# Two attention layers on one core: warm-up products on the raw image, and a stage's statistics spread over six steps

## The chip, the cores and the metric

The kernel runs on one core of one Trainium2 chip. The metric is the device time of one execution in microseconds (us). A core has five engines with queues of their own: TensorE (PE in the profile, with its weight loads shown apart as PEld), VectorE (DVE), ScalarE (ACT), GpSimd (POOL) and SyncE (SP, which only issues transfers here). Each works through its own list of instructions; they meet through semaphores. All arithmetic is fp32.

## The reference, cut to what matters

Four images of 32 x 32 pixels and 768 channels pass through two attention layers. Before each layer the image is normalised over groups of channels, and that normalisation is what the change touches:

```
def _gn(v, G=32, eps=1e-5):
    B_, H_, W_, C_ = v.shape
    g = v.reshape(B_, H_, W_, G, C_ // G)
    m = jnp.mean(g, axis=(1, 2, 4), keepdims=True)
    s = jnp.var(g, axis=(1, 2, 4), keepdims=True)
    return ((g - m) / jnp.sqrt(s + eps)).reshape(v.shape)
...
x = x + _L0_conv_ref(_gn(x), ...)
x = x + _L1_conv_ref(_gn(x), ...)
```

`_L0_conv_ref` is attention with 12 heads of 64 channels over the 1024 pixels, with a relative position bias from rows and columns, between projections (q, k, v and the output). `_L1_conv_ref` is the same, with a 3 x 3 depthwise convolution and a layer norm on q, k and v ahead of the scores.

## The kernel before

**Stages, items and steps.** A stage is one layer of one image; there are eight, in the order image 0 layer 0, image 1 layer 0, image 0 layer 1, image 1 layer 1, and then the same for images 2 and 3. A stage has six items, a pair of heads each. `attend` (L700) makes the attention of one item: for each of two halves of the queries (`c`) it goes twice over four tiles of 128 keys (`g`). For such a group PE makes four tiles of scores (L785 q by k, L787 the bias added), ACT takes their exponentials into `e` (L792), and PE multiplies them with v (L809). In layer 0 DVE also adds the four `e` into `acc` (L801, L803), whose column sums PE makes later (`z`, L754); in layer 1 the sums come out of the product with v itself.

**Who orders the work.** Nothing is scheduled by the compiler on PE, DVE, ACT and POOL: each engine executes in the order in which the program is written. `attend` is a generator which yields twice after a group's scores, exponentials and additions, and twice after its products with v. Each yield is a step; an item has 16. Everything else (the next item's projections, the convolution's taps, weight sums, the next image's normalisation) is cut into pieces which `at(step, piece)` hangs on steps (L943); the loop at L1001 writes the pieces of a step between two parts of `attend`. A step thus sets a place in every engine's list, and not a time: engines reach their parts of one step at different times.

In one item the steps 8 and 9 come after the scores of the third group, 10 and 11 after its products with v, 12 and 13 after the scores (and, in layer 0, the four additions to `acc`) of the fourth group, and 14 and 15 after that group's products with v.

**The normalisation.** `group_norm` (L301) is a generator too. For each of six slices `xn[:, n, :]` of the image (128 partitions x 1024) it issues two `bn_stats` on DVE (L307), 512 columns each. `bn_aggr` makes mean and variance per partition from them (L311, tile `mv`). A PE product with a constant matrix averages over the four partitions of a channel group (L316, `gn_mean`); DVE copies it out of PSUM (L318, `gmean`) and makes the group's variance term (L320, L321, `gd`), PE averages that (L325, `gn_var`), DVE adds epsilon (L327), and ACT and DVE make one over the root (L153 to L160). Last, six DVE instructions normalise the image in place (L337).

For the first image the whole generator runs ahead of the loop (L994). For the other seven stages, `k` = 1 to 7, it runs in the third item of the stage before (L952): twelve calls, three steps apart, from step 2 of that item on. The generator before yields after slices 1 and 3, after the aggregate, and again idly, so that the steps of that item are

| part | step |
|---|---|
| `bn_stats` of slices 0, 1 (four instructions) | 2 |
| slices 2, 3 (four) | 5 |
| slices 4, 5 (four) and the aggregate | 8 |
| mean product L316, L318 to L321 | 14 |
| variance product L325, L327 | 20 |
| one over the root | 23 |
| normalising, two slices each | 26, 29, 32 |

For `k` = 1, 2, 5, 6 the surrounding stage is of layer 0, for `k` = 3, 4, 7 of layer 1.

**The start.** The first image comes in as six transfers, one a slice (L228). Behind the variance product PE executes five "warm" products (L333) of the identity with a constant of 384 columns, whose result nobody reads; then the first projection (L131, `qkv`) waits for the normalised slices. A full fp32 product shows in the trace as two matmul records and two weight loads.

Of the kernel before, what the change touches and what calls it, by code (L numbers as in the profile page):

```python
# [9 lines left out]
F32 = mybir.dt.float32  # L10
# [3 lines left out]
ALU = mybir.AluOpType  # L14
# [3 lines left out]
P = 128  # L18
# [4 lines left out]
NC = C // P  # L23
# [5 lines left out]
EPS = 1e-5  # L29
# [16 lines left out]
def two_layers(ctx: ExitStack, tc: tile.TileContext, keep, x_in, wqkv, wproj, rels, windows, vrow, small, const, onehot, picks, out):  # L46
# [19 lines left out]
    nc = tc.nc  # L66
# [8 lines left out]
    ps_a = pool("ps_a", 1, space=PSUM)  # L75
# [49 lines left out]
    def small_bank(name):  # L125
        return ps_small.tile([P, 512], F32, tag="small", name=name)
# [14 lines left out]
    cst = fixed.tile([P, NCONST], F32, tag="cst", name="cst")  # L141
    nc.sync.dma_start(cst, const)
    ident = cst[:, IDENT : IDENT + P]
# [6 lines left out]
    def rsqrt(v, n, name):  # L150

        ln = stat.tile([P, n], F32, tag=f"ln{n}", name=f"ln_{name}")
        nc.scalar.activation(ln, v, AF.Ln)  # L153
        r = stat.tile([P, n], F32, tag=f"r{n}", name=f"r_{name}")
        nc.scalar.activation(r, ln, AF.Exp, scale=-0.5)
        t = stat.tile([P, n], F32, tag=f"t{n}", name=f"t_{name}")
        nc.vector.tensor_mul(t, r, r)
        nc.vector.tensor_mul(t, t, v)
        nc.vector.tensor_scalar(t, t, -0.5, 1.5, ALU.mult, ALU.add)
        nc.vector.tensor_mul(r, r, t)  # L160
        return r


    stages = [(b0 + k, layer) for b0 in range(0, B, 2) for layer in range(2) for k in range(2)]
# [42 lines left out]
    def shift(i):  # L207

        return 4 if i and items[i][1] == 0 and items[i - 1][1] == 1 else 0
# [3 lines left out]
    for i, (_, layer, hp) in enumerate(items):  # L213
        first = (i - 1) * 16 + shift(i)
# [8 lines left out]
    def load_xn(stage):  # L223
        b, layer = stage
        xn = xnp.tile([P, NC, T], F32, tag=f"xn{stages.index(stage) % 2}", name="xn")
        src = rows(mid[b] if layer else x_in[b])
        for n in range(NC):
            nc.sync.dma_start(xn[:, n, :], src[:, n, :])  # L228
        xns[stage] = xn
# [60 lines left out]
    def mix_tokens(stage):  # L290


        x11, x12, x21, x22 = (xns[stage][:, n : n + 3, h : h + HALF] for n in (0, 3) for h in (0, HALF))
        for to, x, y, op in (
            (quarters[1], x11, x12, ALU.add), (x12, x12, x22, ALU.subtract), (quarters[2], x21, x22, ALU.add),
            (x21, x21, x11, ALU.subtract), (quarters[0], x11, x22, ALU.add),
        ):
            nc.vector.tensor_tensor(to, x, y, op)
            yield

    def group_norm(stage):  # L301

        xn = xns[stage]
        st = stat.tile([P, NC * 2, 6], F32, tag="bn", name="bn", bufs=1)
        for n in range(NC):
            for h in range(2):
                nc.vector.bn_stats(st[:, 2 * n + h, :], xn[:, n, h * HALF : (h + 1) * HALF])  # L307
            if n in (1, 3):
                yield
        mv = stat.tile([P, 2], F32, tag="mv", name="mv")  # L310
        nc.vector.bn_aggr(mv, st.rearrange("p a b -> p (a b)"))  # L311
        yield
        yield
        group = cst[:, GROUP : GROUP + P]
        ps = small_bank("gn_mean")
        nc.tensor.matmul(ps[:, 0:1], group, mv[:, 0:1], start=True, stop=True)  # L316
        mean = stat.tile([P, 1], F32, tag="gmean", name="gmean")
        nc.vector.tensor_copy(mean, ps[:, 0:1])  # L318
        d = stat.tile([P, 1], F32, tag="gd", name="gd")
        nc.vector.tensor_sub(d, mv[:, 0:1], mean)  # L320
        nc.vector.scalar_tensor_tensor(d, d, d, mv[:, 1:2], ALU.mult, ALU.add)  # L321
        yield
        yield
        ps = small_bank("gn_var")
        nc.tensor.matmul(ps[:, 0:1], group, d, start=True, stop=True)  # L325
        v = stat.tile([P, 1], F32, tag="gv", name="gv")
        nc.vector.tensor_scalar(v, ps[:, 0:1], EPS, None, ALU.add)  # L327
        yield
        if stage == stages[0]:

            ps = small_bank("warm")
            for _ in range(5):
                nc.tensor.matmul(ps[:, : 3 * P], ident, cst[:, : 3 * P], start=True, stop=True)  # L333
        r = rsqrt(v, 1, "gn")
        yield
        for n in range(NC):
            nc.vector.tensor_scalar(xn[:, n, :], xn[:, n, :], mean, r, ALU.subtract, ALU.mult)  # L337
            if n % 2:
                yield
# [603 lines left out]
    def at(step, piece):  # L943
        events.setdefault(step, []).append(piece)

    n_steps = NKT * (T // QC)
    oss = [[] for _ in stages]
    for k in range(1, len(stages)):
        first = (k - 1) * NC * n_steps
        at(first + n_steps + 4, lambda k=k: load_xn(stages[k]))  # L950
        norm = group_norm(stages[k])
        for r in range(12):  # L952
            at(first + 2 * n_steps + 2 + 3 * r, lambda norm=norm: next(norm, None))
        if stages[k][1] == 0:
            mix = mix_tokens(stages[k])
            for r in range(5):
                step = 5 * n_steps + r // 3 if stages[k - 1][1] else 4 * n_steps + 4 + r // 2
                at(first + step, lambda mix=mix: next(mix, None))
        elif stages[k - 1][1] == 0:
            at(first + 4 * n_steps + 6, lambda: [nc.gpsimd.memset(pad, 0.0) for pad in pads])  # L960
# [17 lines left out]
    for k, stage in enumerate(stages):  # L978
        call, sums, products = project(stage, oss[k])
        first = (k + 1) * NC * n_steps  # L980
# [13 lines left out]
    for _ in group_norm(stages[0]):  # L994
        pass
# [330 lines left out]
```

## Time and profile before

| | |
|---|---|
| time, median of 3 runs | 3866.32 us (3866.01 to 3870.61) |
| profiled execution, its own time | 3867.89 us |
| its span (first to last instruction) | 3866.1 us |
| ACT busy | 1793.1 us (46%) |
| DVE busy | 2468.8 us (64%) |
| POOL busy | 477.8 us (12%) |
| scores, L785 and L787, PE busy | 815.7 and 615.2 us |
| projections and the like, L131, PE busy | 814.3 us |
| products with v, L809, PE busy | 598.0 us |
| additions to `acc`, L803, DVE | 360.1 us, 1225 ns each |
| `bn_stats`, L307, DVE | 96 instructions, median 677 ns |
| aggregate, L311, DVE | 8 instructions, median 480 ns |

How to read it: a group of instructions stands with its line in the kernel, its engine, what it writes and reads (out<-in), how many there are, their busy time and mean, and the engine's idle time just ahead of them with what ended it. A timeline row has the start in the span, the duration from the first start to the last end of the merged instructions, and in brackets the idle time ahead of the row. On DVE a row's duration overlaps the next row's by some 0.1 us, so that costs are better taken from one start to the next. The profile also has the clock that TensorE was granted, as a share of full speed.

### The profile page before, as it was taken

The page shows a single profiled execution, that of the slowest core. Times are in us where ns is not written, and L with a number is a line of the kernel's source. Part 1 is how long each engine was busy: PE and PEld are TensorE (multiplying, and loading weights), DVE is VectorE, ACT ScalarE, POOL GpSimd, SP SyncE. Part 2 cuts the span into 40 slices and gives each one's busy share as a digit, 9 for nine tenths or more (in the row PEclk, how much of TensorE's full clock was granted, in tenths as well). Part 3 has the DMA queues.
Part 4 walks back from the last instruction along what each step waited for, and adds up shares of the span by engine and source line. Part 5 has one row for each costly group of instructions (what it writes and reads, how often), then busy time and mean ns, then how long its engine had stood idle before and what let it go on. Part 6 is the DMA issues. An engine that isn't in the chain of part 4 may idle for free. (4 is left out here: it accounts for less than half of the span.)

```text
span 3866.1 us, 76044 instructions
## 1 busy us (share of the span) xinstructions
PE 3780.0 (98%) x32988; PEld 1646.0 (43%) x32988; DVE 2468.8 (64%) x3068; ACT 1793.1 (46%) x2573; POOL 477.8 (12%) x870
## 2 busy tenths in 40 slices
PE   8999999999999999999899999999999999999998
PEld 3535535533334443344435445355343444434432
DVE  2566454559588876788354554455685887857774
ACT  2455434545255553456334544254452555525551
POOL 0111100111111211111100010011111121111120
PEclk9999999999999999999999999999999999999999
DMA  4344452321431213311234132522124121142123
GB/s 150 104 121 116 130 159 73 108 71 42 123 96 46 69 43 112 109 45 45 74 113 123 52 77 62 173 62 74 43 55 151 54 66 48 47 123 64 48 53 99
DMA packets 211013, 330.61 MB, mean 86 GB/s; under 512 B 47570, under 2 KB 100562, under 8 KB 210672
## 3 DMA queue, kind: packets, MB, share of 16 engines
q1 hardware_dynamic: 122912, 212.26, 17.6%
q0 software_dynamic: 87760, 113.40, 12.3%
q8 instruction: 263, 4.31, 0.5%
q14 instruction: 78, 0.64, 0.1%
HBM read 184.62 MB, written 40.10 MB: 58 GB/s over the span
## 5 line engine op out<-in xcount | busy, mean ns | idle before, releaser
L792 ACT ACTIVATE e<-s 128x1024 f32<-128x1024 f32 x768 | 773.7, 1024 | 420.9 <-PE s L787 392.4
L785 PE MATMUL s<-q,k 64*128 64x512 f32 x3072 | 815.7, 608 | 18.3 <-ACT e L792 16.6
L131 PE MATMUL qkv<-xn,wqkv_t 128*64 128x512 f32 x3648 | 814.3, 595 | 2.6 <-DVE gmean L318 2.6
L531 DVE SCALAR_TENSOR_TENSOR shared<-shared,sm 128x1056 f32<-128x1056 f32 x576 | 758.1, 1316 | 15.6
L787 PE MATMUL s<-bias,ones 64*128 64x512 f32 x1536 | 615.2, 795 | 14.0 <-DMA bias<-whole 10.2
L809 PE MATMUL av<-e,vt 128*64 128x512 f32 x2624 | 598.0, 597 | 0.0
L627 POOL DMA_DIRECT2D bias<-high x384 | 205.0, 549 | 2174.0 <-ACT high L616 1936.8
L131 PEld LDWEIGHTS qkv<-xn,wqkv_t 128*64 128x64 f32 x3648 | 251.3, 137 | 490.5 <-issue 485.2
L803 DVE TENSOR_TENSOR acc<-acc,e 128x1024 f32<-128x1024 f32 x294 | 360.1, 1225 | 113.7 <-ACT e L792 87.0
L785 PEld LDWEIGHTS s<-q,k 64*128 64x128 f32 x3072 | 281.2, 188 | 279.1 <-issue 208.8
L514 ACT ACTIVATE shared<-qkv,sm 128x512 f32<-128x512 f32 (+1 forms) x288 | 129.3, 502 | 501.3 <-PE qkv L131 501.3
L809 PEld LDWEIGHTS av<-e,vt 128*64 128x64 f32 x2624 | 182.0, 137 | 353.0 <-issue 318.9
L787 PEld LDWEIGHTS s<-bias,ones 64*128 64x128 f32 x1536 | 149.8, 189 | 202.2 <-issue 185.0
L627 POOL DMA_DIRECT2D bias<-whole x384 | 206.2, 560 | 58.4 <-DVE whole L617 45.7
L801 DVE TENSOR_TENSOR acc<-e 128x1024 f32<-128x1024 f32 x49 | 60.0, 1225 | 226.9 <-ACT e L792 216.8
L722 ACT COPY weighed<-av 128x512 f32<-128x512 f32 x96 | 56.4, 587 | 276.9 <-PE av L809 276.9
L546 DVE TENSOR_REDUCE mean<-ln_c 128x8 f32<-128x512 f32 x144 | 98.5, 684 | 117.1 <-PE ln_c L543 117.1
L600 PEld LDWEIGHTS rel<-q,rel 64*32 64x32 f32 x6144 | 112.0, 106 | 78.1 <-issue 72.7
L728 POOL DMA_DIRECT2D z<-weighed x47 | 26.9, 573 | 919.5 <-ACT weighed L722 514.0
L557 DVE TENSOR_REDUCE lnv<-shared 128x16 f32<-128x1024 f32 x72 | 87.6, 1216 | 69.4 <-ACT shared L553 69.4
L600 PE MATMUL rel<-q_t,rel 64*32 64x32 f32 x6144 | 123.6, 195 | 4.2 <-issue 4.2
L399 DVE TENSOR_TENSOR shared<-shared,m3m 128x512 f32<-128x512 f32 x66 | 45.4, 687 | 128.7 <-PE m3m L131 128.4
(158 smaller groups left out, 4471.3 us busy)
## 6 DMA issues: line engine op xcount, KB each, us to landing
bias<-high POOLq DMA_DIRECT2D x384, 128.0 KB, 2.9
bias<-whole POOLq DMA_DIRECT2D x384, 128.0 KB, 3.0
wqkv_t<-in_wqkv SPq DMA_DIRECT2D x78, 384.0 KB, 3.2
wqkv_t<-mixed SPq DMA_DIRECT2D x66, 384.0 KB, 3.1
wproj_t<-mixed SPq DMA_DIRECT2D x48, 384.0 KB, 3.3
wqkv_t<-in_wqkv SPq DMA_DIRECT2D x66, 192.0 KB, 2.5
xn<-in_x SPq DMA_DIRECT2D x24, 512.0 KB, 8.3
x<-in_x SPq DMA_DIRECT2D x48, 256.0 KB, 3.3
```

Of the source, the lines that this page charges most:

```text
L131: nc.tensor.matmul(ps[lo : lo + D], a[:, lo : lo + D], b, start=start, stop=stop, **kw)
L514: nc.scalar.activation(self.pad[s][:, rows, there : there + src.shape[2]], src, AF.Identity, bias=col(self.column(s)))
L531: nc.vector.scalar_tensor_tensor(y, window, tap, y, ALU.mult, ALU.add)
L546: nc.vector.tensor_reduce(of, heads, AX.X, ALU.add)
L557: nc.vector.tensor_reduce(v, squared.rearrange("p (a d) -> p a d", d=D), AX.X, ALU.add)
L600: nc.tensor.matmul(ps[lo : lo + S, k * S : (k + 1) * S].rearrange("p (b c) -> p b c", b=2), rel[rows, 2 * self.layer + i, first : first + ...
L627: nc.gpsimd.dma_start(sets, some.unsqueeze(1).to_broadcast([D // 2, 2, QC]))
L785: nc.tensor.matmul(ps[:, j, :], k[rows, keys], q[rows, cols], start=True, stop=False)
L787: nc.tensor.matmul(ps[:, j, :], ones[rows, keys], bias[c][rows, kt // 2, :], start=False, stop=True,)
L792: nc.scalar.activation(e, ps, AF.Exp)
L803: nc.vector.tensor_tensor(acc, acc, e, ALU.add)
L809: nc.tensor.matmul(av[j * D : (j + 1) * D, :], pair.vt[:, kt, j * D : (j + 1) * D], e[:, j, :], start=(kt == 0), stop=(kt == NKT - 1),)
```

## The change

In `group_norm` the generator now yields after each of the slices 0 to 4, so that the statistics run in six calls of two `bn_stats`, the last one with the aggregate; the two idle yields are gone. The list of steps on which the calls hang is written out. The result: slices 0 to 5 on steps 2, 4, 6, 8, 10 and 12 of the item, the aggregate with slice 5 on step 12 (it was on step 8); mean, variance, root and normalising stay on steps 14, 20, 23, 26, 29, 32.

For the first image the five warm products move and change: three are issued behind the statistics of slice 4 and read that slice of the raw image (so they wait for its transfer), one stands between mean product and variance product, two stand behind the variance product. They are six, and write into a bank of the scores' pool instead of the small bank.

```
             for h in range(2):
                 nc.vector.bn_stats(st[:, 2 * n + h, :], xn[:, n, h * HALF : (h + 1) * HALF])
-            if n in (1, 3):
+            if stage == stages[0] and n == NC - 2:
+
+                ps = ps_a.tile([P, 2, 512], F32, tag="a", name="warm")
+
+                def warm(n):
+                    for _ in range(n):
+                        nc.tensor.matmul(ps[:, 0, : 3 * P], ident, xn[:, NC - 2, : 3 * P], start=True, stop=True)
+
+                warm(3)
+            if n < NC - 1:
                 yield
         mv = stat.tile([P, 2], F32, tag="mv", name="mv")
         nc.vector.bn_aggr(mv, st.rearrange("p a b -> p (a b)"))
         yield
-        yield
         group = cst[:, GROUP : GROUP + P]
-        ps = small_bank("gn_mean")
-        nc.tensor.matmul(ps[:, 0:1], group, mv[:, 0:1], start=True, stop=True)
+        small = small_bank("gn_mean")
+        nc.tensor.matmul(small[:, 0:1], group, mv[:, 0:1], start=True, stop=True)
+        if stage == stages[0]:
+            warm(1)
...
         nc.vector.scalar_tensor_tensor(d, d, d, mv[:, 1:2], ALU.mult, ALU.add)
         yield
-        yield
...
         if stage == stages[0]:
-
-            ps = small_bank("warm")
-            for _ in range(5):
-                nc.tensor.matmul(ps[:, : 3 * P], ident, cst[:, : 3 * P], start=True, stop=True)
+            warm(2)
         r = rsqrt(v, 1, "gn")
...
         norm = group_norm(stages[k])
-        for r in range(12):
-            at(first + 2 * n_steps + 2 + 3 * r, lambda norm=norm: next(norm, None))
+        for r in (0, 2, 4, 6, 8, 10, 12, 18, 21, 24, 27, 30):
+            at(first + 2 * n_steps + 2 + r, lambda norm=norm: next(norm, None))
```

More of the change, by code (lines that the diff above doesn't have):

```diff
@@ L312, in group_norm @@
         yield
-        yield
         group = cst[:, GROUP : GROUP + P]
-        ps = small_bank("gn_mean")
-        nc.tensor.matmul(ps[:, 0:1], group, mv[:, 0:1], start=True, stop=True)
+        small = small_bank("gn_mean")
+        nc.tensor.matmul(small[:, 0:1], group, mv[:, 0:1], start=True, stop=True)
+        if stage == stages[0]:
+            warm(1)
         mean = stat.tile([P, 1], F32, tag="gmean", name="gmean")
-        nc.vector.tensor_copy(mean, ps[:, 0:1])
+        nc.vector.tensor_copy(mean, small[:, 0:1])
         d = stat.tile([P, 1], F32, tag="gd", name="gd")
@@ L322, in group_norm @@
         yield
-        yield
-        ps = small_bank("gn_var")
-        nc.tensor.matmul(ps[:, 0:1], group, d, start=True, stop=True)
+        small = small_bank("gn_var")
+        nc.tensor.matmul(small[:, 0:1], group, d, start=True, stop=True)
         v = stat.tile([P, 1], F32, tag="gv", name="gv")
-        nc.vector.tensor_scalar(v, ps[:, 0:1], EPS, None, ALU.add)
+        nc.vector.tensor_scalar(v, small[:, 0:1], EPS, None, ALU.add)
         yield
         if stage == stages[0]:
-            ps = small_bank("warm")
-            for _ in range(5):
-                nc.tensor.matmul(ps[:, : 3 * P], ident, cst[:, : 3 * P], start=True, stop=True)
+            warm(2)
         r = rsqrt(v, 1, "gn")
```

## The prediction, on record before the changed kernel ran

> **What bounds the kernel now.** I read the page's busy times first, then PE's waits, then the timeline around the two places that the change touches.
>
> ```profile
> PE 3780.0 (98%) x32988; PEld 1646.0 (43%) x32988; DVE 2468.8 (64%) x3068; ACT 1793.1 (46%) x2573; POOL 477.8 (12%) x870
> ```
>
> PE is busy for 3780.0 of 3866.1 us, idle for 86. That alone doesn't prove it the bound, so I looked at what its idle time waits for (engine, line, who released it: total us, times, longest):
>
> ```profile
> PE gn_mean L316 <- DVE mv L311: 17.2, 1, 17.2
> ...
> PE qkv L131 <- DVE gmean L318: 2.6, 3, 0.9
> ```
>
> The first is the start of the program. The statistics cost PE nothing later: `gn_mean` never waits again. Second row: the copy of the mean is late for the next projection three times (at 1197, 1702 and 3113, all in layer 1 stages). Now the place of the seven later normalisations, first stage; PE's timeline, then DVE's:
>
> ```profile
> 252.77 3.65 PE L809 MATMUL av<-e,vt 128*64 128x512 f32 x16
> 256.35 0.38 PE L316 MATMUL gn_mean<-mv,cst 128*128 128x1 f32 x2
> 256.67 1.13 PE L785 MATMUL s<-q,k 64*128 64x512 f32 x4
> ```
>
> ```profile
> 247.41 2.46 DVE L307 BATCH_NORM_STATS2 bn<-xn 128x6 f32<-128x512 f32 x4
> 249.90 0.48 DVE L311 BATCH_NORM_AGGREGATE mv<-bn 128x2 f32<-128x72 f32 x1
> 250.30 0.63 DVE L765 SCALAR_TENSOR_TENSOR t<-t,inv 128x512 f32<-128x512 f32 x1
> ...
> 252.30 1.22 DVE L617 TENSOR_TENSOR whole<-whole,high 128x1024 f32<-128x1024 f32 x1
> 253.43 5.21 DVE L803 TENSOR_TENSOR acc<-acc,e 128x1024 f32<-128x1024 f32 x4
> 258.55 0.15 DVE L318 COPY gmean<-gn_mean 128x1 f32<-128x1 f32 x1
> ```
>
> No row has a bracket: neither engine idles. From 212 to 300 PE has no gap at all, so here a PE delay lengthens the program. And DVE is behind PE: PE's mean product is at 256.35, DVE reaches the same step at 258.55. The product has its aggregate at 250.38, 6 us early, only because the aggregate stands on step 8.
>
> The start, all engines:
>
> ```profile
> 12.75 1.29 DVE L307 BATCH_NORM_STATS2 bn<-xn 128x6 f32<-128x512 f32 x2 [0.20 <-DMA xn<-in_x]
> ...
> 19.37 5.35 PE L333 MATMUL warm<-cst 128*128 128x384 f32 x10 [0.25 <-DVE gv L327]
> ...
> 20.83 4.43 DVE L337 TENSOR_SCALAR xn<-xn,gmean,r_gn 128x1024 f32<-128x1024 f32 x6
> ...
> 24.66 15.67 PE L131 MATMUL qkv<-xn,wqkv_t 128*64 128x512 f32 x72
> ```
>
> The first slice is normalised by 21.57 (six in 4.43, so 0.74 each), but PE is in the warm products until 24.65.
>
> [...] weight loads of the warm products are 0.64 us apart up to 22.74, and 0.32 at the end (the recorded full clock begins at 23.16). [...] Windows (from:to, length, busy us and count by engine, granted clock, DMA):
>
> ```profile
> 1820.00:1825.40 5.40, 3.40 (x216) 2.21 (x216) 5.26 (x5) 3.77 (x8) 0.00 (x0) 1.00 0.05 17
> 1825.40:1828.80 3.40, 3.40 (x65) 2.21 (x66) 3.33 (x5) 3.31 (x6) 0.00 (x0) 0.50 0.02 5
> 1842.50:1849.20 6.70, 6.12 (x20) 3.18 (x20) 6.11 (x9) 3.36 (x5) 3.66 (x7) 0.50 0.74 176
> ```
>
> A gap of 2.00 us before 1825.32 was followed by 3.4 us at 0.50; the gap of 3.80 before 1843.08 by 6.8 us at 0.50, from 0.6 before its end. Gaps of 1.57 (1535), 1.76 (880) and one of 2.21 (1860) left the clock full.
> [...] At the start load and product of `gn_mean` both wait until 17.25[...].
> [...] The DVE rows above run in the order of the program.
>
> **The change, part by part.**
>
> *Statistics while a layer 0 stage runs (k = 1, 2, 5, 6).* In DVE's list, slices 4, 5 and the aggregate leave the place after the third group's additions; slice 3 stays there; slice 4 goes between L772 and L617; slice 5 and the aggregate go behind the four additions of the fourth group, immediately ahead of L318. No transfers hang on them; the lists of ACT, POOL and SP stay as they are, and PE's changes at the start alone. From one start to the next, four `bn_stats` and the step to the aggregate take 2.49 (247.41 to 249.90), two in front of an aggregate therefore 1.30 (1.2, and 0.1 for its wait).
> At 247.41: two `bn_stats` (1.23, half of 2.46) and the aggregate (0.40, from 249.90 to 250.30) are gone: L765 starts 1.63 earlier, at 248.7. Slice 4 takes back 1.2, so L617 and the additions start 0.43 earlier, at 253.0; their exponentials (ACT 249.62 to 253.91) are in time for that. The additions take 5.12 from start to next start: 258.12. Slice 5: 259.42. Aggregate 0.48: 259.90; 0.06 from aggregate to product, as at the start (17.19 to 17.25): **`gn_mean` starts at 259.96 instead of 256.35, and PE waits 3.6 us**.
> The same arithmetic elsewhere: L318 follows PE's product by 2.20 (697.13, 699.33), 2.19 (2173.85, 2176.04) and 2.18 (2613.62, 2615.80), with the same rows ahead, so the wait is 2.2 - 0.43 + 1.84 = 3.6 at each. Behind the waiting product are the next item's scores, `z` and all projections; ACT waits for those scores, DVE for `z`. PE has no gap for 130 us behind the first of these places (the next is 0.94 at 387), so nothing is caught up: **4 x 3.6 = 14.4**.
>
> *The clock after such a wait.* This is not shown for a 3.6 us gap at these places. From below: no drop, 0. From above: two windows at half clock as after the 3.80 gap, of which 6.2 us lay behind its end: 3.1 lost. Between: one window, 1.7 lost. [...] I take 2.0 each: **+8.0** (0 to 12.4).
>
> *Statistics while a layer 1 stage runs (k = 3, 4, 7).* The aggregate was done at 1164.56 for a product at 1195.21. On step 12 it stands ahead of L157 of the K norm, where DVE idles 3.15 us (up to 1186.82, for ACT); two `bn_stats` and an aggregate are 1.8, and DVE arrives earlier by the 1.7 that left step 8 less the 1.2 of step 10. Covered. If that cover were gone, the copy L318 would be up to 1.8 later, 5.4 in all. The wait of 1.34 on ACT at 1159.93 (again at 1665 and 3076) comes from `lnv` on DVE, ahead of which stand four `bn_stats` before (step 5) and four after (steps 4 and 6): it stays. **0.**
>
> *The start.* Slice 4 arrives at some 12.7. Three warm products are six passes of 0.64: until 16.6, before the mean product (17.25), which isn't delayed. The fourth (two passes, 0.64 at full or 1.28 at half clock) begins at some 17.7 and can hold the variance product (18.54) by up to 0.4. Two more begin at 19.37 and end at 20.7 (full) or 21.9 (half). The projection can start when slice 0 is ready, 21.6; its weights were issued at 10.0 and 11.3 and landed within 9.3, by 20.3. At full clock it gains 24.65 - 21.6 = 3.05, and slices come each 0.74, faster than PE uses them (four records of 0.215, 0.86). If the clock is half until 23.16 as before: 1.5 + half of 1.26 = 2.1. Reading raw slice 4 holds its normalising (24th us) for nothing. I take **-2.6** (-1.5 to -3.1).
>
> *Sum.* Against the profiled span: 3866.1 + 14.4 + 8.0 - 2.6 = 3885.9. The profiled execution took 3867.89 in all, 1.8 outside the span, and the median of the runs is 3866.32, so the sum on the median is 3866.3 + 19.8 = **3886**; its own range, with the clock loss from 0.8 to 3.1 a place, 3880 to 3893.
>
> **Rivals.**
> A. The waits come, the clock stays full (as after the 2.21 gap at 1860): 3866.3 + 14.4 - 2.6 = 3878. Against it: seven gaps from 1.9 us up dropped it.
> B, the other side. The aggregate isn't late: DVE gets to step 12 at least 3.6 us sooner, and the mean product finds `mv` ready. It decides at one point, aggregate done before PE's 256.3. For it: 2.4 us of DVE idle time before 243.60. Against it: that idle time ends with an event that follows PE, and behind it DVE runs without a gap up to 258.55. The stats would then cost nothing and the start gives 3866.3 - 2.6 = 3863.7, not slower.
> C. As B, and the shorter DVE pieces also end the three waits of 1.34 and of 0.88 in layer 1: 3863.7 - 6.7 = 3857. Against it: DVE's list ahead of both is as long as before.
> D. The change doesn't warm PE early[...]: that is the 2.1 above, within the range.
>
> **How the numbers follow.** Forecast 0.72, A 0.14, B 0.08, C 0.02, and 0.04 for something larger than 3893. The range 3876 to 3893 takes in forecast and A, less some edges: about 0.82. A measurement tells about 0.2% (7.7 us) from no change: B lies within that, C is faster, forecast and A are slower: 0.02, 0.08, 0.90.
>
> **What would show it.** Right: four waits of `gn_mean` on DVE `mv`, 3.6 each, at some 254, 700, 2182 and 2628, none in layer 1; granted clock 0.5 for 3 to 7 us behind most of them; the first projection at 21 to 23. The copy L318 then follows the product at once instead of 2.2 behind. Wrong: no such waits, or waits that PE makes up for before the stage ends, or new gaps at L131 behind `gmean` in layer 1.

## The result and the profile after

| | before | after |
|---|---|---|
| time, median of 6 runs each | 3866.44 us (3865.80 to 3870.61) | 3891.15 us (3888.52 to 3892.34) |
| profiled execution, its own time | 3867.89 us | 3891.77 us |
| its span | 3866.1 us | 3889.9 us |

The changed kernel is slower: ratio 1.0061, with a 95% interval of 1.0048 to 1.0074. The forecast was 3886, range 3876 to 3893. In what follows L324 of the changed kernel is `gn_mean` (L316 before), L320 the aggregate (L311), L791 the scores (L785), L815 the products with v (L809).

The page of the kernel after, its first line and PE's part of the busy times:

```profile
span 3889.9 us, 76047 instructions
PE 3792.8 (98%) x32990; PEld 1653.1 (42%) x32990; DVE 2469.4 (63%) x3068; ACT 1791.9 (46%) x2573; POOL 477.9 (12%) x870
```

PE has two records more and is busy for 12.8 us longer (3792.8 less 3780.0), while DVE's and ACT's busy times hardly moved. The span grew by 23.8, so another 11 us of it are idle time of PE. PE's waits after (PE's instruction <- the one that it waited for: us in total, times, longest):

```profile
PE s L791 <- ACT e L798: 17.9, 8, 5.1
PE gn_mean L324 <- DVE mv L320: 14.0, 4, 3.5
...
PE qkv L131 <- DVE gmean L328: 2.6, 3, 0.9
...
PE qkv L131 <- DVE xn L343: 1.5, 1, 1.5
```

Before, `gn_mean` waited once, at the start. Now it waits four times for 3.5 us each, at 255.83, 703.76, 2188.38 and 2634.62, which are the four places with a layer 0 stage around them. The three waits for `gmean` in layer 1 are as they were. The first of the four places, PE's timeline and then DVE's:

```profile
248.66 3.65 PE L815 MATMUL av<-e,vt 128*64 128x512 f32 x16
255.83 0.58 PE L324 MATMUL gn_mean<-mv,cst 128*128 128x1 f32 x2 [3.51 <-DVE mv L320]
256.34 2.08 PE L791 MATMUL s<-q,k 64*128 64x512 f32 x4
```

```profile
248.86 5.21 DVE L809 TENSOR_TENSOR acc<-acc,e 128x1024 f32<-128x1024 f32 x4
253.98 1.28 DVE L307 BATCH_NORM_STATS2 bn<-xn 128x6 f32<-128x512 f32 x2
255.29 0.48 DVE L320 BATCH_NORM_AGGREGATE mv<-bn 128x2 f32<-128x72 f32 x1
256.45 0.16 DVE L328 COPY gmean<-gn_mean 128x1 f32<-128x1 f32 x1 [0.68 <-PE gn_mean L324]
```

DVE comes straight out of the four additions to `acc` into the last two statistics and the aggregate, and PE, which has long been at the mean product, waits until the aggregate ends at 255.77. The copy, which was 2.20 us behind its product, now follows it at once and is the one that waits. The four scores behind the product took 1.13 before and take 2.08 now: the clock has dropped. Four stretches behind those waits (from:to, length, busy us and count of PE, PEld, DVE, ACT and POOL, granted clock, DMA share, GB/s):

```profile
255.70:262.50 6.80, 6.67 (x20) 3.37 (x22) 3.13 (x9) 2.05 (x2) 0.00 (x0) 0.50 0.62 199
702.80:709.60 6.80, 5.83 (x18) 3.05 (x20) 1.41 (x5) 1.67 (x2) 0.60 (x2) 0.50 0.34 88
2187.60:2194.40 6.80, 6.03 (x20) 3.24 (x20) 1.22 (x5) 1.86 (x2) 0.40 (x1) 0.50 0.31 78
2634.80:2638.20 3.40, 3.40 (x12) 1.75 (x14) 0.54 (x3) 0.65 (x1) 0.00 (x0) 0.50 0.28 74
```

Half clock for 6.8 us at three places and for 3.4 at the fourth. The start, PE's timeline:

```profile
12.24 4.18 PE L314 MATMUL warm<-xn,cst 128*128 128x384 f32 x6 [12.24 <-DMA xn<-in_x]
...
17.57 1.54 PE L314 MATMUL warm<-xn,cst 128*128 128x384 f32 x4
20.64 0.65 PE L131 MATMUL qkv<-xn,wqkv_t 128*64 128x512 f32 x2 [1.53 <-DVE xn L343]
```

The four last records of the warm products take 1.54 us, 0.385 each, where the six first took 4.18, 0.70 each: the clock is full from 16.78 on. The first projection begins at 20.64 instead of 24.66. It waits for its normalised slice now and no longer for the warm products.

Where the 23.8 us come from, measured by the distance between the same instructions in both traces:

| part | us |
|---|---|
| start, up to the first projection | -4.0 |
| waits of `gn_mean` at four places, 3.51 + 3.51 + 3.50 + 3.50 | +14.0 |
| PE's way from mean to variance product there, 31.96, 31.99, 31.94, 31.94 before; 35.12, 34.73, 34.82, 33.52 after | +10.4 |
| three layer 1 places (the scores' wait of 1.34 grew to 1.48, 1.81, 1.47) | +0.7 |
| elsewhere: about 1.1 where the image pairs change and behind it (1830 to 2100), about 0.9 from 3740 on, and small steps of up to 0.4 | +2.7 |

### The profile page after: what moved, and what is told of

It is laid out like the page before. It is cut to its first block, busy times and chain, and to the rows that moved or that the text cites. A ratio compares the mean times of both kernels' runs of the same rounds, so it can differ in the third digit from the quotient of the medians.

```text
span 3889.9 us, 76047 instructions
## 1 busy us (share of the span) xinstructions
PE 3792.8 (98%) x32990; PEld 1653.1 (42%) x32990; DVE 2469.4 (63%) x3068; ACT 1791.9 (46%) x2573; POOL 477.9 (12%) x870
## 5 line engine op out<-in xcount | busy, mean ns | idle before, releaser
L791 PE MATMUL s<-q,k 64*128 64x512 f32 x3072 | 824.3, 614 | 19.6 <-ACT e L798 17.9
L815 PE MATMUL av<-e,vt 128*64 128x512 f32 x2624 | 597.7, 598 | 0.0
L809 DVE TENSOR_TENSOR acc<-acc,e 128x1024 f32<-128x1024 f32 x294 | 360.2, 1225 | 113.9 <-ACT e L798 87.3
L791 PEld LDWEIGHTS s<-q,k 64*128 64x128 f32 x3072 | 284.2, 190 | 283.1 <-issue 210.0
L815 PEld LDWEIGHTS av<-e,vt 128*64 128x64 f32 x2624 | 181.5, 137 | 352.5 <-issue 318.8
```

Of the source, the lines that this page charges most:

```text
L791: nc.tensor.matmul(ps[:, j, :], k[rows, keys], q[rows, cols], start=True, stop=False)
L809: nc.vector.tensor_tensor(acc, acc, e, ALU.add)
L815: nc.tensor.matmul(av[j * D : (j + 1) * D, :], pair.vt[:, kt, j * D : (j + 1) * D], e[:, j, :], start=(kt == 0), stop=(kt == NKT - 1),)
```

## The experiments

The theory is that of the prediction: the aggregate is last in DVE's list ahead of the mean product, behind additions that DVE reaches late; PE waits 3.5 us four times, and the clock drop behind the waits costs another 10.4 in all. The rivals: the new start costs something later; the small pieces as such are what delays; the clock drop belongs to the place and not to the gap. All kernels compute the whole output. Their edits are against the changed kernel. What a place costs is the growth, against the kernel before, of PE's way from the last product ahead of the place to the variance product behind it, in the profiled executions. A ratio is to the kernel before, in runs of the same chip; there its median was 3868.68 (first four), 3868.47 (next four) and 3870.58 (last two).

**1. The spread statistics alone.** The warm products stand as before.

```
-            if stage == stages[0] and n == NC - 2:
...
-                warm(3)
...
-            warm(2)
+            ps = small_bank("warm")
+            for _ in range(5):
+                nc.tensor.matmul(ps[:, : 3 * P], ident, cst[:, : 3 * P], start=True, stop=True)
```

> Only the statistics are spread over the six steps; the warm products at the start are those of before. Theory (the mean product waits for the late aggregate at four places in layer 0 stages, and the half clock follows): four waits of 3.5 us and some 10 us of lost clock, nothing gained at the start: 3866.4 + 24 = 3890 to 3894 us, the first projection at 24 to 25 us. Rival (the warm products in the scores' bank cost as well): clearly less than the changed kernel's 3891, some 3880.

Measured: 3893.21 us, ratio 1.0063 (1.0047 to 1.0078). PE's waits (five, the longest is the start):

```profile
PE gn_mean L315 <- DVE mv L311: 30.2, 5, 16.1
```

30.2 - 16.1 = 14.1 at four places, with half clock of 6.8, 6.8, 6.8 and 3.4 us behind them. The whole loss is there without the new start, so the start has no part in it.

**2. The new start alone.** Statistics four at a time on steps 2, 5 and 8 again, aggregate on 8.

```
-            if n < NC - 1:
+            if n in (1, 3):
...
-        for r in (0, 2, 4, 6, 8, 10, 12, 18, 21, 24, 27, 30):
+        for r in (0, 3, 6, 12, 18, 21, 24, 27, 30):
```

> Only the warm products are changed; the statistics run four at a time on steps 2, 5 and 8 as before. Theory: no wait of the mean product in any later stage, the first projection at 20.6 to 21.7 us instead of 24.66, so 3866.4 - 3 to 4 = 3862.4 to 3863.4 us. Rival (the start gives its gain back at a later wait): 3866 us.

Measured: 3867.03, ratio 0.9994 (0.9986 to 1.0003). `gn_mean` doesn't wait after the start. The first projection is at 21.90, 2.7 us sooner than before, with the aggregate as late as before (16.81, 16.71). The trace shows the gain of the start, of which 2.0 us are left at the end of the program; the time alone can't be told from no change, and it is above the forecast.

**3. Two at a time, but early.** Slices on steps 2, 3, 4, 5, 6 and the last with the aggregate on 8.

```
-        for r in (0, 2, 4, 6, 8, 10, 12, 18, 21, 24, 27, 30):
+        for r in (0, 1, 2, 3, 4, 6, 12, 18, 21, 24, 27, 30):
```

> The changed kernel with the same pieces of two statistics each, but on steps 2, 3, 4, 5, 6 and 8, so that the aggregate is on step 8 as before. Theory (the aggregate's place alone decides): no wait of the mean product, 3862.4 to 3863.4 us as with the warm products alone. Rival (cutting the statistics into pieces of two costs by itself): 3870 us or more.

Measured: 3873.06, ratio 1.0011 (1.0005 to 1.0018), so the expected gain isn't there, and the time is the one that the rival forecast; experiment 7 decides between them. The waits of `gn_mean` are gone, and the four places are within 0.11 us of the kernel before, as expected. The miss is in the three layer 1 stages. PE's timeline at the first of them, before and here, and the stretch behind it:

```profile
1159.93 1.13 PE L785 MATMUL s<-q,k 64*128 64x512 f32 x4 [1.34 <-ACT e L792]
```

```profile
1158.77 1.84 PE L791 MATMUL s<-q,k 64*128 64x512 f32 x4 [2.53 <-ACT e L798]
```

```profile
1159.10:1162.50 3.40, 3.40 (x14) 1.88 (x10) 3.33 (x6) 2.47 (x3) 0.45 (x1) 0.50 0.15 29
```

The wait of 1.34 has become 2.53, and now drops the clock; three such places cost 8.3 us. The chain of the wait: ACT's `ln_ln` waits for DVE's `lnv`, and the exponentials that free PE's score banks stand behind `ln_ln` in ACT's list. Six statistics stood ahead of `lnv` (step 6) here and four before; ACT's idle time ahead of `ln_ln` grew from 2.74 to 3.93, by 1.19, which is two `bn_stats`.

**4. The mean product moved too.** From step 14 to 16, which puts it behind the products with v, the next scores and `z`.

```
-        for r in (0, 2, 4, 6, 8, 10, 12, 18, 21, 24, 27, 30):
+        for r in (0, 2, 4, 6, 8, 10, 14, 18, 21, 24, 27, 30):
```

> The changed kernel with the statistics left on steps 2 to 12, but the mean product two steps later, on step 16, behind the next item's first scores. Theory: the aggregate, ready at some 255.8 us, is then in time (PE comes to the product at some 257 us or later), no gap of 3.5 us and no half clock at the four places: 3862 to 3865 us. Rival (spreading costs wherever PE waits, and another wait takes the place of this one): 3875 us or more.

Measured: 3868.86, ratio 0.9998 (0.999 to 1.0007): well under the rival, but over the forecast. PE's timeline:

```profile
258.95 0.38 PE L324 MATMUL gn_mean<-mv,cst 128*128 128x1 f32 x2 [0.79 <-ACT t L761]
```

The statistics stay exactly where the change put them, and the wait of 3.5 and the half clock are gone. A smaller wait stands in its place, 0.79 until ACT has read the result of `z`, which has just filled the bank that the small products share; the places are 0.91 to 0.96 us over the kernel before. In layer 1 the three waits for `gmean` of 0.88 went.

**5. The gap filled.** Four full products, whose result nobody reads, ahead of each `gn_mean` with a layer 0 stage around it.

```
         small = small_bank("gn_mean")
+        if stage in stages[1:] and stages[stages.index(stage) - 1][1] == 0:
+            for _ in range(4):
+                nc.tensor.matmul(small, ident, cst[:, :512], start=True, stop=True)
```

> The changed kernel with four idle products of 512 columns (constants, result unread) ahead of the mean product at the four places in layer 0 stages: 4 x 0.85 = 3.4 us, about as long as the wait, so that PE is busy instead of idle. Theory (the wait costs 14.0 us by itself and the half clock behind it some 10): no drop of the clock at the four places, PE's delay there 3.5 to 3.9 us each instead of 7.0, 6.3, 6.6 and 5.2, total 3891 - 10 = 3879 to 3883 us. Rival (the clock loss is no loss, other engines need the time to start again after a wait): 3891 us as before.

Measured: 3880.10, ratio 1.0033 (1.002 to 1.0046). PE's timeline (`gn_mean` is L327 here), then the clock over the same place (columns as above):

```profile
251.50 3.65 PE L818 MATMUL av<-e,vt 128*64 128x512 f32 x16
255.08 3.70 PE L326 MATMUL gn_mean<-cst 128*128 128x512 f32 x8
258.67 0.38 PE L327 MATMUL gn_mean<-mv,cst 128*128 128x1 f32 x2
```

```profile
255.00:258.50 3.50, 3.50 (x10) 1.44 (x8) 3.36 (x5) 0.59 (x1) 3.30 (x7) 1.00 0.93 238
258.50:262.00 3.50, 3.50 (x21) 1.93 (x20) 2.88 (x9) 1.56 (x2) 0.00 (x0) 1.00 0.64 174
```

PE has no gap and keeps full clock, yet is delayed by 3.50, 3.48, 3.51 and 3.52 us, 14.0 in all: just the wait, as the aggregate still ends only at 258.61. So the 10.4 us behind the waits are the clock's, and they belong to the gap. By spans this kernel is 7.6 us under the changed one (3882.3, 3889.9), although its profiled execution was the longest of its five. The places give 14.0 + 10.4 - 14.0 = 10.4, and the start takes 2.7 back: there the gap ahead of the first projection was 1.98 and the clock fell for 3.4 us from 22.3.

**6. The aggregate alone late.** Statistics four at a time on 2, 5, 8 as before; only the aggregate goes to step 12.

```
-            if n < NC - 1:
+            if n in (1, 3, 5):
...
-        for r in (0, 2, 4, 6, 8, 10, 12, 18, 21, 24, 27, 30):
+        for r in (0, 3, 6, 10, 12, 18, 21, 24, 27, 30):
```

> The warm products of the changed kernel; the statistics four at a time on steps 2, 5 and 8 as in the kernel before, and the aggregate alone moved to step 12, behind the additions. Theory (the aggregate's place): DVE's additions end at 258.15 on the clock of the kernel before, the aggregate at 258.66, so PE waits 2.3 to 2.4 us at each of the four places, with a drop of the clock at most of them: 3863.5 + 9.5 + 4 to 7 = 3873 to 3881 us. Rival (small pieces of statistics are what costs): no wait, 3863 us.

Measured: 3878.71, ratio 1.0028 (1.0017 to 1.0038). PE's timeline:

```profile
255.32 0.38 PE L324 MATMUL gn_mean<-mv,cst 128*128 128x1 f32 x2 [2.19 <-DVE mv L320]
255.63 1.42 PE L791 MATMUL s<-q,k 64*128 64x512 f32 x4
```

2.19, 2.19, 2.18, 2.17 at the four places, 8.7 in all, with 3.4 us of half clock behind each (1.6 lost each). The places are 3.85, 3.79, 3.87 and 3.87 us over the kernel before: an aggregate of half a microsecond in the wrong place costs some 15 us, without any small pieces. The last two `bn_stats` are the other 1.3 us of each wait.

**7. Early, and out of `lnv`'s way.** Slices on steps 2, 3, 7, 8, 9, and the last with the aggregate on 10.

```
-        for r in (0, 2, 4, 6, 8, 10, 12, 18, 21, 24, 27, 30):
+        for r in (0, 1, 5, 6, 7, 8, 12, 18, 21, 24, 27, 30):
```

> The changed kernel with the statistics, two at a time, on steps 2, 3, 7, 8, 9 and 10: the aggregate stays ahead of the additions of the fourth group, and in layer 1 stages nothing stands between steps 4 and 6, ahead of the lnv that ACT and PE wait for. Theory: no wait of the mean product, and the three waits of 1.3 us at the scores of layer 1 stages (at 1158, 1663 and 3074 us) go: 3863.5 - 4 = 3859 to 3861 us, ratio 0.998. Rival (pieces of two cost by themselves): 3866 us or more.

Measured: 3865.66, ratio 0.9994 (0.9986 to 1.0002), over the forecast and just under the rival's. No wait of `gn_mean` after the start, and in layer 1 the scores' wait is gone: 1.63 us at each of three stages. A new one appeared in layer 0, four times about 1.0:

```profile
254.73 0.50 PE L793 MATMUL s<-bias,ones 64*128 64x512 f32 x2 [1.02 <-DMA bias<-whole]
```

DVE prepares the next bias (`whole`, L623) at 249.44, behind the statistics of steps 8 to 10, instead of 247.73 in the changed kernel; the transfer of it is late for the scores. That gives back 1.20 to 1.25 at each place. So the pieces of two themselves cost nothing in layer 1, where the scores' wait went with them in place; what is lost is lost to the bias, as experiment 9 shows.

**8. The same, and the mean product at step 16 in layer 1 alone.**

```
+        for r in (0, 1, 5, 6, 7, 8, 14 if stages[k - 1][1] else 12, 18, 21, 24, 27, 30):
```

> As the kernel with statistics on steps 2, 3, 7, 8, 9 and 10, and the mean product on step 16 where the surrounding stage is of layer 1 (14 elsewhere). Theory: the three waits of 0.88 us of a projection for the copy of the mean go as well, 1.2 us each by the run with the late mean product: 3 to 4 us less than without, 3856 to 3858 us. Rival (another wait takes their place): no difference.

Measured: 3863.53, ratio 0.9989 (0.9981 to 0.9997): 2.1 us under experiment 7 where 3 to 4 were forecast. The waits for `gmean` are gone too, so that each of the three layer 1 stages is about 2.5 us shorter than in the kernel before; the bias waits of 0.95 to 0.99 in layer 0 stay.

**9. A list for each layer.** Layer 1 as in 8, layer 0 as in 3.

```
+        for r in (0, 1, 5, 6, 7, 8, 14, 18, 21, 24, 27, 30) if stages[k - 1][1] else (0, 1, 2, 3, 4, 6, 12, 18, 21, 24, 27, 30):
```

> Steps by the layer of the surrounding stage: in layer 1 as in the kernel before this one (statistics on 2, 3, 7, 8, 9, 10, mean product on 16), in layer 0 statistics on 2, 3, 4, 5, 6, 8 and mean product on 14, so that nothing stands ahead of the split of the bias that the transfers wait for. Theory: the four waits of 1.0 us for the bias transfers (1.3 us each in PE's time) go, no other comes: 3863.5 - 5 = 3857 to 3860 us, ratio 0.9975. Rival (the split is late for another reason): 3863 us.

Measured: 3858.80, ratio 0.9968 (0.9956 to 0.998), faster than the kernel before and so than the changed one. The layer 0 places stand within 0.11 us of the kernel before and have no bias wait, layer 1 gains 2.49, 2.05 and 2.48. The start gains 0.8 only. PE's wait there, and the stretch behind it:

```profile
PE qkv L131 <- DVE xn L343: 2.1, 1, 2.1
```

```profile
22.70:26.10 3.40, 3.40 (x12) 1.03 (x10) 3.04 (x5) 0.00 (x0) 0.00 (x0) 0.50 1.02 408
```

The two warm products end too soon: the gap of 2.14 ahead of the first projection is again followed by 3.4 us at half clock.

**10. Four warm products behind the variance product instead of two**, otherwise as 9.

```
-            warm(2)
+            warm(4)
```

> As the kernel with steps by layer, with four warm products instead of two behind the variance product, so that PE idles 0.3 to 0.9 us instead of 1 to 2 us ahead of the first projection. Theory: with the gap gone the clock can't drop ahead of the first projection, as it did in the run with the filled wait (3.4 us at half clock from 22.3): up to 1.5 us less in runs where it drops, none in others, no loss. Rival (at half clock the four products last 2.6 us longer and delay the projection): up to 1.5 us more.

Measured: 3857.67, ratio 0.996 (0.9946 to 0.9973). The gap ahead of the first projection is 0.22 and the clock stays up. Its interval overlaps that of 9, so the times don't separate the two; the trace shows the drop at the start gone. One more drop appeared elsewhere: a gap of 1.76 at 876 was followed by 3.4 us at half clock, while a gap of the same length in the kernel before (880) kept it full; the last section sets the two side by side.

## Why the prediction was right, step by step

- *Statistics while a layer 0 stage runs.* Forecast 4 x 3.6 = 14.4, measured 14.0. The aggregate was to end at 259.90; it ended at 255.77, which is 259.9 with the 4.11 us added by which PE's work ahead of the place stood earlier. Experiments 4 and 6 confirm the reason: moving the consumer behind the aggregate takes the wait away, moving the aggregate alone brings 2.2 of it. PE's record is empty in each gap of 3.5 us, so all its work behind the product came later by it.
- *The clock after such a wait.* Right in kind at all four places, small in size: 8.0 against 10.4 (3.16, 2.74, 2.88, 1.58). That the clock would drop at all was an estimate, from the seven drops behind gaps of 1.9 us and more in the trace of the kernel before. The 2.0 was one too, a middle between 3.4 us of half clock, as behind the gap of 2.00 there, and 6.8, as behind that of 3.80; three of four places had 6.8. That is the mis-sized term. The loss is 0.46 or 0.47 of the half-clock time that lay behind each gap (6.71, 5.93, 6.10 and 3.41 us). Experiment 5 shows that this is the price of the gap: the same delay without a gap costs nothing more.
- *Statistics while a layer 1 stage runs.* Forecast 0, measured 0.7. The same four statistics stand ahead of `lnv`, as worked out; the three waits for `gmean` didn't change. But the scores' wait did not quite stay: it is 1.48, 1.81 and 1.47 in the changed kernel, the same within 0.01 in experiments 1, 4 and 5, which keep the statistics on its steps, and 1.34 or 1.35 in 2 and 6, which don't. So the growth belongs to the spread pieces; why one wait grew by 0.46 stays open.
- *The start.* Forecast -2.6, measured -4.0. The slices landed 1.28 us sooner in the profiled execution (aggregate at 15.43, before 16.71), which is no effect of the change: the other executions put it between 15.4 and 16.9, with and without it. From the aggregate to the first projection it is 7.95 before, 5.21 after, 5.09 in experiment 2 and 8.07 in experiment 1. The gain proper is 2.7 to 2.9 by these pairs; over all nine profiled executions with the new start and two last products the stretch is 4.4 to 5.5.
- *The sum.* +19.8 forecast, +23.8 in the trace, +24.7 in the medians. The 2.4 of the clock and 3.4 in layer 1 and elsewhere were missing, and 1.4 at the start and 0.4 of the waits lay on the other side. That the trace comes as near as it does to the sum is in part luck, as 1.3 of the start is the earlier arrival of the image. The 2.7 elsewhere stays unexplained.
- *Rivals.* A (full clock) falls with the recorded half clock; B and C (aggregate in time) with the four waits; D (no early warming) with the full clock from 16.78 on. What C hoped for in layer 1 can be had, but by moving the statistics away from `lnv` (experiments 7 to 10), which the change doesn't do.
- *The gap and the drop.* Gaps of 2.17 to 2.19 were followed by half clock four times of four (experiment 6), the one of 2.21 at 1860 of the kernel before was not. Behind equal gaps of 3.5 the clock was at half for 6.8 us three times and for 3.4 once; the last section shows where those gaps lie among the recorded changes of the clock.

## What to carry to other kernels

In a hand-ordered program a step is a place in each engine's list and not a time: before work is moved to a later step, compare when its engine gets there with when the consumer's engine does. Here DVE was 2.2 us behind PE at the step that the aggregate was moved ahead of, and that lag plus the moved work is the wait. Here a wait of PE of 2.2 to 3.5 us cost its length and another 1.6 to 3.2 for the clock. Moving the consumer later removed this wait (experiment 4), though another stood at the new place (0.79 for the bank). And smaller pieces gave nothing by themselves: what counts is which small instruction that others wait for (`lnv`, `whole`, the aggregate) they stand in front of.

## What the runs showed of the hardware

The first three points are counted in the recorded clock and PE's matmul records of two profiled executions, that of the kernel before and that of the changed one; no run varied them on purpose.

- All recorded changes of the clock in one trace, 16 in the kernel before and 26 in the changed one, lie multiples of 3.41 us apart, to within 0.003 us. In the changed kernel 255.71, 262.54, 702.86 and 709.68 are 2, 129 and 2 times 3.41 apart.
- The two traces, divided into stretches of 3.41 us that begin where changes are recorded or multiples of it away: at full clock all 19 stretches in which PE was idle for 1.86 us or more were followed by half clock, and none of the 2207 with 1.81 or less. The length of a gap alone did not tell: one of 2.21 at 1860 of the kernel before lay with 1.76 in one stretch and 0.45 in the next, and the clock stayed full. The gap of 1.76 in experiment 10 lay in one stretch (first row: PE busy for 1.65 of 3.41) and was followed by half clock; in the kernel before it was split (second row; columns as above) and the clock stayed. At 888 of the changed kernel a gap of 1.76 inside one stretch left it full too, so these runs show no sharp limit.

```profile
875.73:879.14 3.41, 1.65 (x10) 0.67 (x10) 3.24 (x8) 2.86 (x5) 0.00 (x0) 1.00 0.00 0
876.49:879.91 3.42, 2.23 (x14) 0.84 (x10) 3.38 (x4) 0.83 (x3) 0.00 (x0) 1.00 0.00 0
```

- At half clock all 18 stretches without idle time of PE were followed by full clock, one of the 4 with 0.12 to 0.63 us of it, and none of the 7 with more. At the four places of the changed kernel the three drops that began before the gap ended (at 255.71, 702.86 and 2187.65, with `gn_mean` at 255.83, 703.76 and 2188.38) lasted 6.83 us, the one that began behind it (2634.80, with `gn_mean` at 2634.62) 3.41. The first of the four: an idle stretch, then one with 0.12 idle at half clock, behind which half clock went on for another.

```profile
252.30:255.71 3.41, 0.02 (x2) 0.00 (x0) 3.27 (x5) 0.59 (x1) 3.16 (x7) 1.00 0.95 246
255.71:259.12 3.41, 3.29 (x10) 2.01 (x12) 2.59 (x9) 0.24 (x1) 0.00 (x0) 0.50 0.58 163
```

- The arrival of the first image varied by some 1.5 us from one execution to the next (aggregate at 15.4 to 16.9), half as much as the start's gain: times from the start are to be compared from the aggregate on.
